# A selective-scan kernel: operand addresses on GpSimd, and a fixed order of products and scans on VectorE

## The chip, the core and the metric

The kernel runs on one core of a Trainium2 chip. A core has engines that work side by side, each through its own queue in order: TensorE (matrix products, PE in the profile), VectorE (DVE), ScalarE (ACT), GpSimd (POOL) and SyncE (SP), which issues transfers. They share a memory of 128 partitions, from which and to which the transfers go, and PSUM, into which TensorE writes and which VectorE and ScalarE read. The metric is the time of one execution on the device in microseconds; lower is better.

## What is computed

Two layers of a vision model on `x`, of shape (2, 96, 96, 96). The change lies in layer 0. There, after a normalisation over the channels, an input projection makes 192 channels of `xin` and a gate `z`; a 3x3 convolution, a GELU and a 1x1 convolution give an offset at each pixel, at which `xin` is sampled bilinearly. The sampled image is cut into windows of 36 tokens, and over each a selective scan runs in four directions, with 16 states to each channel:

```python
def step(hst, inputs):
    ut, dt, bt, ct = inputs
    dA = jnp.exp(dt[..., None] * A)
    hst = hst * dA + (dt * ut)[..., None] * bt[:, :, None, :]
    y = jnp.einsum('bkdn,bkn->bkd', hst, ct)
    return (hst, y)
...
return jnp.moveaxis(ys, 0, -1) + Dv[None, :, :, None] * u
```

The four outputs are summed, normalised, multiplied with `silu(z)` and projected; a small feed-forward net with quantised weights follows. Layer 1 (an attention against averaged cells, a 5x5 depthwise convolution and another such net) is the same before and after.

## The kernel before

Layer 0 goes over the two images in 32 stripes of 6 rows (576 tokens). For each stripe there are three parts. The front (`_l0_front`) loads, normalises, projects, convolves, samples, and writes the step sizes `dl`, the products `du` of step and input, and the C coefficients `c_d` to device memory, from where they are read again with each row laid out over partitions. The scan (`_l0_scan`) is next, and the back (`_l0_back`) does the rest. Front of the next stripe, scan of this one and back of the one before run interleaved.

The scan of a stripe has 2 halves of the channels, 2 orders of the tokens (`o`) and 2 directions (`kk`), each a section (`_l0_section`); a section has 4 quarters `i` of the states, and a quarter two units `c`, each of 288 tokens. So there are 1024 quarters and 2048 units in all. A quarter first loads `cre` (C, repeated over partitions) and has ScalarE make `dA` for both units in three decays (L1041, 3072 in all). Each unit then takes five steps:

- spread (L1056, TensorE): B, repeated over partitions, into a `bp` buffer in PSUM; there are two such buffers
- product (L1060, VectorE): `bp` becomes `dur` times B, 864 elements a partition. The product of the first unit also waits by hand for the three decays of its quarter, and for GpSimd and TensorE to be done with the `h` buffers that this quarter will write
- scan (L1076, VectorE): the recurrence over `dA` and `bp`, into one of six `h` buffers. When it has ended, the `bp` buffer is free for a later spread
- times C (L1081, GpSimd): `h` times `cre`, in place
- fold (L1093, TensorE): sums `h` over states into `y`; three matmuls for the first unit and six for the second.

The same GpSimd queue holds, for each stripe, fourteen steps of the sampling (L625 to L631, `sample`), twenty-four of the softplus and the product `du` (L759 to L762, in `steps`, three for each of two orders), their marks (`memset`), and two products with `zs` and a sum in the back (L937, L883).

The order of the work is planned as the program is built. `_Plan` records each operation with an engine, an estimated cost, what it reads and writes, and a due time; `order` then picks, again and again, the operation that can start earliest, with due time as second key. An operation that needs one of another engine is taken to be ready a fixed time (`LAG`) after that one's end, by the engine that is to run it: 1.5 us for VectorE. The instructions of each engine stay in that order on the chip. The costs of GpSimd come from `_cost` and, for times C, from a number of its own.

A tile may be given `skip`: `_place` then takes a buffer longer by `lead` (or `skip`) elements and starts the tile `skip` elements in, that is 4 bytes each after an aligned place. Before, `h` has skip 2, 4, 8 or 1 by quarter, `zs` 12, `x1` 14, `x2` 9, and `e`, `du`, `r` and `dl` 0, 1, 2 and 6:

```python
ht = S.tile(P.rep, [128, NBL, H2], "h", P.nh, skip=(2, 4, 8, 1)[i], lead=8)
```

`cre` has none. Nothing fixes the order of products and scans but the plan: 1814 of the 2048 scans stand between their own product and another product.

Of the kernel before, what the change touches and what calls it, by code (L numbers as in the profile page):

```python
# [9 lines left out]
F32 = mybir.dt.float32  # L10
# [4 lines left out]
ALU = mybir.AluOpType  # L15
# [11 lines left out]
C = 96  # L27
HW = 96
# [62 lines left out]
class _Op:  # L91
    def __init__(self, eng, cost, run, due, tab):
        self.eng, self.cost, self.run, self.due, self.tab = eng, cost, run, due, tab
        self.deps, self.tiles, self.start, self.end = set(), [], None, None
        self.left, self.then, self.ready = 0, [], 0.0

SAME = 0.06  # L100
LAG = {"pe": 0.5, "dve": 1.5, "act": 0.6, "pool": 1.0, "sp": 1.5}


class _Plan:
# [6 lines left out]

    def tile(self, pool, shape, tag, bufs=1, dtype=F32, name=None, skip=None, lead=0):
        t = _Tile(self, pool, tag, bufs, shape, dtype, name or tag)
        t.skip, t.lead = skip, lead or skip
        return t
# [30 lines left out]
    def order(self):  # L146
# [13 lines left out]
        while len(out) < len(self.ops):  # L160
# [70 lines left out]
def _place(t, tag):  # L231

    if t.skip is None:
        return t.pool.tile(t.shape, t.dtype, tag=tag, name=t.name, bufs=1)
    n = math.prod(t.shape[1:])
    flat = t.pool.tile([t.shape[0], n + t.lead], t.dtype, tag=tag, name=t.name, bufs=1)
# [223 lines left out]
def _l0_front(k, P, S, f, x, b, s, at):  # L460
# [25 lines left out]

    xt, xin = temp([C, 8, HW], "xt"), S.tile(P.front, [C, 2, 8, HW + 2], "xin", 1)
    if lo > r0:
# [9 lines left out]
    )  # L498
    pool(8, lambda: nc.gpsimd.memset(xin.ap[:, :, :, 0 : HW + 2 : HW + 1], 0.0), (), (xin,))
    rows = lambda t, c: t.ap[:, 4 * c : 4 * c + 4, :].rearrange("p r w -> p (r w)")  # L500
# [41 lines left out]

    zs = f.zs = S.tile(P.hand, [C, 2, T], "zs", 2, skip=12)

# [17 lines left out]
    def convolve(oh, c):  # L562
        pc = ps("pc")

        def part(ih, tap):
            dy, dx = divmod(tap, 3)
            pe(H2, lambda: nc.tensor.matmul(  # L567
                pc.ap[:C, :H2],
                k.w_c1[:, ih, tap, oh * C : (oh + 1) * C],
                xin.ap[:, ih, 3 * c + dy : 3 * c + dy + 3, dx : dx + HW],  # L570
                start=(ih == 0 and tap == 0),
                stop=(ih == 1 and tap == 8),
            ), (xin,), (pc,), (t,))
# [14 lines left out]

    fr = temp([C, 2, WIN, HW], "fr", 5)

# [24 lines left out]
    xs1 = S.tile(P.front, [C, 2, T], "xs1", 1)  # L615
    dif, top, bot = temp([C, 2, 7, HW], "dif"), temp([C, 2, WIN, HW], "top", 2), temp([C, 2, WIN, HW], "bot")
    g = nc.gpsimd
    tt = g.tensor_tensor

    def sample(half):  # L620
        v = lambda: xin.ap[:, half, 1:8, 1 : HW + 1]
# [3 lines left out]
        pool(672, lambda: tt(d(), xin.ap[:, half, 1:8, 2 : HW + 2], v(), ALU.subtract), (xin,), (D,))  # L625
        pool(T, lambda: tt(tp(), d()[:, 0:6], fx(), ALU.mult), (D, (fr, 1)), (TP,))
# [35 lines left out]
    def order_of(o, xs):  # L662
# [50 lines left out]

        x1, x2 = row("x1", 1, skip=14), row("x2", 1, skip=9)

# [14 lines left out]
        def steps(m):  # L730
# [277 lines left out]
def _l0_section(k, P, S, f, first, o, h, kk, py, at, tau):  # L1008
# [41 lines left out]
    def unit(u, i, c, cre, dA, t0):  # L1050
        toks = slice(c * H2, (c + 1) * H2)
        bp = S.tile(P.ps, [128, 1024], "bp", 2)
        ht = S.tile(P.rep, [128, NBL, H2], "h", P.nh, skip=(2, 4, 8, 1)[i], lead=8)

# [16 lines left out]
        def scan():  # L1071
            hv, dv = (v.rearrange("p b n -> p (b n)") for v in (ht.ap, dA.ap[:, c]))
            bv = bp.ap[:, : NBL * H2]
            if kk:
                hv, dv, bv = hv[:, ::-1], dv[:, ::-1], bv[:, ::-1]
            nc.vector.tensor_tensor_scan(hv, dv, bv, 0.0, ALU.mult, ALU.add)  # L1076

        S.op("dve", 2.0, scan, (dA, bp), (ht,), due=t0 + (1.35 - P.early["dve"]) * tau)

        def times_c():  # L1080
            nc.gpsimd.tensor_tensor(  # L1081
                ht.ap, ht.ap, cre.ap[:, toks].unsqueeze(1).to_broadcast([128, NBL, H2]), ALU.mult)
            P.issued["pool", u] = latest()

        S.op("pool", 2.06, times_c, (cre,), (ht,), due=t0 + (2.3 - P.early["pool"]) * tau)

        def states():
            end = o == 1 and kk == 1 and i == NQ - 1

            def part(dst, v, stop):  # L1090
                if o:
                    v = v.rearrange("p (w j i) -> p w i j", i=WIN, j=WIN)
                nc.tensor.matmul(dst, k.fold, v, start=False, stop=stop)  # L1093

            for blk in range(NBL):
                dst = py.ap[CB * blk : CB * blk + CB]
                n = HEAD - H2 if c else H2
                part(dst[:, c * H2 : c * H2 + n], ht.ap[:, blk, :n], end and c == 1)
            if c:
                for blk in range(NBL):  # L1100
                    part(_tail(py, blk), ht.ap[:, blk, n:], end and blk == NBL - 1)
            P.issued["pe", u] = latest()

        S.op("pe", 1.0, states, (ht,), (py,), due=t0 + (3.5 - P.early["pe"]) * tau)

# [4 lines left out]
def _layer0(k, tc, a, x, x2d):  # L1110
# [3 lines left out]
    with ExitStack() as st:  # L1114
# [852 lines left out]
```

## Time and profile before

| | |
|---|---|
| three runs, us | 8442.23 (median), 8434.59, 8457.52 |
| the profiled execution, us | 8449.37; span 8447.6 |
| granted TensorE clock, mean | 0.907 |
| first product to the end of the last scan | 145.3 to 6391.7 us |
| VectorE busy, 1000 to 6000 us | 96.7 to 97.8 of each 100 |
| GpSimd busy, same | 89.9 to 90.7 |
| TensorE busy, same | 85.8 to 86.9 |
| ScalarE busy, same | 77.1 to 77.9 |
| DMA busy, same | 0.48 to 0.49 |

The page first gives the busy time of each engine with its share of the span; then the span in 40 slices with the busy tenths of each; then the costliest groups of instructions. A group's line names the source line, engine, operation, tiles out and in, shapes and count; after the bar stand busy time in us and the mean of one in ns, then the idle time just before these instructions and what ended most of it. A timeline's line has start, length, engine, line, operation, tiles, shapes and count, and in brackets the idle time before it and its releaser. A line of the table of waits has who waited for whom, the sum in us, the number of times and the longest. A duration can overlap the next instruction's by some tens of ns.

### The profile page before, as it was taken

To read this page: it belongs to the slowest core of one execution; us is meant where nothing else is said; L and a number is where in the kernel's file an instruction comes from. 1 tells how busy PE (TensorE), PEld (TensorE's weight loads), DVE (VectorE), ACT (ScalarE), POOL (GpSimd) and SP (SyncE) were. 2 spreads that over 40 slices of the span, in tenths; PEclk is the share of its full clock that TensorE was granted. 3 is DMA by queue.
4 is the path that set the end of the run, shared out by engine and by line. 5 is a ranking of instruction groups with operands and counts; after the bars stand their busy time and mean duration, and the time that the engine had idled before them with its cause. 6 is when DMAs were issued, how large, how long until landed. Compare 5 with 4: busy or idle time off the path is not lost. (4 is left out here: it accounts for less than half of the span.)

```text
span 8447.6 us, 118902 instructions
## 1 busy us (share of the span) xinstructions
PE 7320.6 (87%) x43653; PEld 3406.4 (40%) x43653; DVE 7806.9 (92%) x5398; ACT 6339.6 (75%) x10688; POOL 5742.1 (68%) x3835
## 2 busy tenths in 40 slices
PE   7888888888888888888888888888857999989998
PEld 4444444444444444444444444444423223542245
DVE  3999999999999999999999999999996998959988
ACT  5777777777777777787777877787745886778867
POOL 4999989888889889999988999999873000110001
PEclk8898989999899889999989998999867999989999
DMA  2444444444444444444444444444442000110001
GB/s 89 142 153 152 152 154 150 149 153 146 148 151 149 149 148 153 155 151 150 155 152 147 149 153 150 152 154 155 147 135 63 3 2 14 36 48 3 2 22 33
DMA packets 339992, 985.62 MB, mean 117 GB/s; under 512 B 50152, under 2 KB 51872, under 8 KB 339104
## 3 DMA queue, kind: packets, MB, share of 16 engines
q1 hardware_dynamic: 337488, 977.74, 37.1%
q8 instruction: 347, 5.69, 0.3%
q14 instruction: 253, 2.07, 0.1%
q10 hardware_dynamic: 1904, 0.12, 0.0%
HBM read 797.19 MB, written 139.25 MB: 111 GB/s over the span
## 5 line engine op out<-in xcount | busy, mean ns | idle before, releaser
L1081 POOL TENSOR_TENSOR h<-h,cre 128x864 f32<-128x864 f32 x2048 | 3965.5, 1947 | 616.1 <-DVE h L1076 357.4
L1076 DVE TENSOR_TENSOR_SCAN h<-dA,bp 128x864 f32<-128x864 f32 x2048 | 3996.8, 1953 | 105.4 <-PE y L1093 27.2
L1041 ACT ACTIVATE dA<-dlr,A 128x576 f32<-128x576 f32 x3072 | 2156.5, 765 | 886.1 <-DVE h L1076 828.6
L1060 DVE TENSOR_TENSOR bp<-dur,bp 128x864 f32<-128x864 f32 x2048 | 2133.6, 1043 | 132.9 <-PE bp L1056 51.1
L1093 PE MATMUL y<-h,fold 128*32 128x288 f32 (+2 forms) x18432 | 1841.2, 446 | 154.4 <-POOL h L1081 152.6
L567 PE MATMUL pc<-xin,off 96*96 96x288 f32 x4608 | 1328.1, 420 | 0.0
L1056 PE MATMUL bp<-bt,selb 128*128 128x288 bf16 x2048 | 644.1, 316 | 700.4 <-DVE h L1076 683.7
L1429 ACT ACTIVATE pr<-sc 128x960 f32<-128x960 f32 (+1 forms) x1080 | 954.0, 937 | 202.8 <-PE sc L1425 182.5
L1093 PEld LDWEIGHTS y<-h,fold 128*32 128x32 f32 x18432 | 755.0, 117 | 857.6 <-issue 376.1
L1509 DVE TENSOR_TENSOR sums<-sums,pr 128x3840 f32<-128x3840 f32 (+1 forms) x240 | 959.0, 3996 | 56.9 <-ACT pr L1429 34.7
L567 PEld LDWEIGHTS pc<-xin,off 96*96 96x96 f32 x4608 | 705.2, 165 | 497.8 <-issue 247.2
L1601 POOL MEMSET vch<- 96x32 f32 x16 | 2.4, 152 | 1304.6 <-DVE dist L1463 1213.4
L1056 PEld LDWEIGHTS <-selb 128*128 128x128 bf16 x2048 | 201.5, 99 | 1455.9 <-DVE h L1076 1231.0
L1425 PE MATMUL sc<-qH,kH 32*128 32x480 f32 (+1 forms) x3240 | 627.2, 602 | 10.4 <-DMA q<-qH 5.6
L1425 PE MATMUL sc<-q,kH 32*128 32x480 f32 (+1 forms) x1080 | 564.7, 602 | 0.0
L1491 PE MATMUL av<-pr,vT 128*32 128x480 f32 (+1 forms) x4320 | 533.4, 564 | 3.6 <-ACT av L1516 3.5
L1682 DVE SCALAR_TENSOR_TENSOR acc<-vch,lepe_w,acc 96x1152 f32<-96x1152 f32 x320 | 469.0, 1466 | 7.9
L1425 PEld LDWEIGHTS sc<-qH,kH 32*128 32x128 f32 x3240 | 219.0, 184 | 419.7 <-issue 223.8
L883 POOL TENSOR_TENSOR x<-x,fy 96x576 f32<-96x576 f32 x32 | 53.3, 1664 | 479.1 <-ACT fy L882 415.1
L740 PE MATMUL pt<-xd,w_dt 96*128 96x288 f32 x768 | 304.1, 492 | 21.7 <-ACT xin L532 10.6
L761 POOL TENSOR_TENSOR dl<-dl,r 128x576 f32<-128x576 f32 x192 | 270.9, 1411 | 9.1 <-ACT dl L758 4.1
L762 POOL TENSOR_TENSOR du<-dl,x 128x576 f32<-128x576 f32 x192 | 271.7, 1415 | 6.6
(270 smaller groups left out, 9902.7 us busy)
## 6 DMA issues: line engine op xcount, KB each, us to landing
cre<-c_d SPq DMA_DIRECT2D x1024, 288.0 KB
dur<-du_d SPq DMA_DIRECT2D x256, 864.0 KB
dlr<-dl_d SPq DMA_DIRECT2D x256, 864.0 KB
x<-xs SPq DMA_DIRECT2D x512, 72.0 KB
du_d<-du SPq DMA_DIRECT2D x128, 288.0 KB
dl_d<-dl SPq DMA_DIRECT2D x128, 288.0 KB
du_d<-du SPq DMA_DIRECT2D x128, 144.0 KB
dl_d<-dl SPq DMA_DIRECT2D x128, 144.0 KB
```

Of the source, the lines that this page charges most:

```text
L567: pe(H2, lambda: nc.tensor.matmul(pc.ap[:C, :H2], k.w_c1[:, ih, tap, oh * C : (oh + 1) * C], xin.ap[:, ih, 3 * c + dy : 3 * c + dy + 3, dx ...
L1041: nc.scalar.activation(dA.ap[:, :, blk, :], dlr.ap[:, blk, :].rearrange("p (c n) -> p c n", c=2), AF.Exp, scale=k.A[:, i, kg, h, blk : blk ...
L1056: nc.tensor.matmul(bp.ap[:, :H2], k.selb[:, kk, i, :], f.bc[o].ap[:, toks], start=True, stop=True)
L1060: nc.vector.tensor_tensor(bp.ap[:, : NBL * H2].rearrange("p (b n) -> p b n", b=NBL)[:, ::-1], dur.ap[:, ::-1, toks], bp.ap[:, :H2].unsquee ...
L1076: nc.vector.tensor_tensor_scan(hv, dv, bv, 0.0, ALU.mult, ALU.add)
L1081: nc.gpsimd.tensor_tensor(ht.ap, ht.ap, cre.ap[:, toks].unsqueeze(1).to_broadcast([128, NBL, H2]), ALU.mult)
L1093: nc.tensor.matmul(dst, k.fold, v, start=False, stop=stop)
L1425: nc.tensor.matmul(two[to // 2][:, to % 2, :n], kH[rows, k0 : k0 + 128], q, start=True, stop=True)
L1429: nc.scalar.activation(pr[:, 2 * i : 2 * i + 2, :n], two[i][:, :, :n], AF.Exp, scale=HD**-0.5)
L1491: nc.tensor.matmul((main if s < HEADS else other)[s * HD : (s + 1) * HD, :n], vT[:, blk, hd, :], pr[:, place(s, p), :n], start=at == 0, st ...
L1509: nc.vector.tensor_tensor(both, both, pr[:, :, :, :n], ALU.add)
L1682: S.op("dve", 1.43, lambda: nc.vector.scalar_tensor_tensor(acc.ap, src(), W.lw[:, t : t + 1], acc.ap, ALU.mult, ALU.add), (vch,), (acc,))
```

## The change

It has two parts. First, the tiles that GpSimd reads in pairs are moved so that the two operands start 8 bytes apart modulo 16 where that can be had: `h` has skip 2 in all quarters, against `cre` with none; `zs`, `x1`, `x2` and `du` have skip 2, `dl` and `e` 0, `r` stays at 2; `fr` and `top` move; `xin` is two columns wider and its pixels begin one column later. In the built program every times C, softplus step, `du` and `zs` product is then at 8 bytes; the sampling steps are at 8, 4 or 12. Before, times C was at 8 bytes in quarter 0, at 0 in quarters 1 and 2 and at 12 in quarter 3. `lead` is gone.

Secondly, each product and scan also writes a token, `P.turn`, in the order in which they are recorded, and a quarter's first scan, times C and fold are recorded only after its second product. So VectorE has product, product, scan, scan in each quarter, and the quarters one after another; other VectorE work may still stand between. The planner's costs change along: product 1.03 to 1.0, times C 2.06 to 1.75, GpSimd's `_cost`, and 0.6 us instead of 1.5 from a spread to its product (`SOON`).

```diff
+SOON = {"dve": 0.6}
...
-                p.ready = max(p.ready, o.end + (SAME if p.eng == o.eng else LAG[p.eng]))
+                p.ready = max(p.ready, o.end + (SAME if p.eng == o.eng else o.lag[p.eng]))
...
-        return 0.1 + 0.00235 * cols
+        return 0.2 + 0.00177 * cols
...
-    xt, xin = temp([C, 8, HW], "xt"), S.tile(P.front, [C, 2, 8, HW + 2], "xin", 1)
+    xt, xin = temp([C, 8, HW], "xt"), S.tile(P.front, [C, 2, 8, HW + 4], "xin", 1)
...
-            xin.ap[:, half, 4 * c : 4 * c + 4, 1 : HW + 1],
+            xin.ap[:, half, 4 * c : 4 * c + 4, 2 : HW + 2],
...
-    zs = f.zs = S.tile(P.hand, [C, 2, T], "zs", 2, skip=12)
+    zs = f.zs = S.tile(P.hand, [C, 2, T], "zs", 2, skip=2)
...
-    fr = temp([C, 2, WIN, HW], "fr", 5)
+    fr = temp([C, 2, WIN, HW], "fr", 2)
...
-    dif, top, bot = temp([C, 2, 7, HW], "dif"), temp([C, 2, WIN, HW], "top", 2), temp([C, 2, WIN, HW], "bot")
+    dif, top, bot = temp([C, 2, 7, HW], "dif"), temp([C, 2, WIN, HW], "top", 1), temp([C, 2, WIN, HW], "bot")
...
-        x1, x2 = row("x1", 1, skip=14), row("x2", 1, skip=9)
+        x1, x2 = row("x1", 1, skip=2), row("x2", 1, skip=2)
...
-            e, du, r, w = (row(name, 2, skip=n) for name, n in (("e", 0), ("du", 1), ("r", 2), ("dl", 6)))
+            e, du, r, w = (row(name, 2, skip=n) for name, n in (("e", 0), ("du", 2), ("r", 2), ("dl", 0)))
...
-        ht = S.tile(P.rep, [128, NBL, H2], "h", P.nh, skip=(2, 4, 8, 1)[i], lead=8)
+        ht = S.tile(P.rep, [128, NBL, H2], "h", P.nh, skip=2)
...
-        S.op("pe", 0.3, spread, (f.bc[o],), (bp,), due=t0 - P.early["pe"] * tau)
-        S.op("dve", 1.03, product, (dur,), (bp,), due=t0 - P.early["dve"] * tau)
...
-        S.op("dve", 2.0, scan, (dA, bp), (ht,), due=t0 + (1.35 - P.early["dve"]) * tau)
...
-        S.op("pool", 2.06, times_c, (cre,), (ht,), due=t0 + (2.3 - P.early["pool"]) * tau)
...
+        S.op("pe", 0.3, spread, (f.bc[o],), (bp,), due=t0 - P.early["pe"] * tau).lag = SOON
+        S.op("dve", 1.0, product, (dur,), (bp, P.turn), due=t0 - P.early["dve"] * tau)
+
+        def rest():
...
+            S.op("dve", 2.0, scan, (dA, bp), (ht, P.turn), due=t0 + (1.35 - P.early["dve"]) * tau)
...
+            S.op("pool", 1.75, times_c, (cre,), (ht,), due=t0 + (2.3 - P.early["pool"]) * tau)
...
+        if c == 0:
+            P.behind = rest
+        else:
+            P.behind()
+            rest()
...
+        P.turn, P.behind = S.held(k.ident, "turn"), None
```

In the built program each engine has as many instructions as before but ScalarE, which has 78 more: loads of function tables, since the plan orders its work otherwise.

More of the change, by code (lines that the diff above doesn't have):

```diff
@@ L110, in __init__, with tile @@
         self.rate = {}
-    def tile(self, pool, shape, tag, bufs=1, dtype=F32, name=None, skip=None, lead=0):
+    def tile(self, pool, shape, tag, bufs=1, dtype=F32, name=None, skip=None):
         t = _Tile(self, pool, tag, bufs, shape, dtype, name or tag)
-        t.skip, t.lead = skip, lead or skip
+        t.skip = skip
         return t
@@ L235, in _place @@
     n = math.prod(t.shape[1:])
[L236 removed]
+    flat = t.pool.tile([t.shape[0], n + t.skip], t.dtype, tag=tag, name=t.name, bufs=1)
     v, d = flat[:, t.skip : t.skip + n], t.shape[1:]
@@ L1104, in unit, with scan, times_c, states @@
-        S.op("pe", 1.0, states, (ht,), (py,), due=t0 + (3.5 - P.early["pe"]) * tau)
+        S.op("pe", 0.3, spread, (f.bc[o],), (bp,), due=t0 - P.early["pe"] * tau).lag = SOON
+        S.op("dve", 1.0, product, (dur,), (bp, P.turn), due=t0 - P.early["dve"] * tau)
+        def rest():
+            def scan():
+                hv, dv = (v.rearrange("p b n -> p (b n)") for v in (ht.ap, dA.ap[:, c]))
+                bv = bp.ap[:, : NBL * H2]
+                if kk:
+                    hv, dv, bv = hv[:, ::-1], dv[:, ::-1], bv[:, ::-1]
+                nc.vector.tensor_tensor_scan(hv, dv, bv, 0.0, ALU.mult, ALU.add)
+            S.op("dve", 2.0, scan, (dA, bp), (ht, P.turn), due=t0 + (1.35 - P.early["dve"]) * tau)
+            def times_c():
+                nc.gpsimd.tensor_tensor(
+                    ht.ap, ht.ap, cre.ap[:, toks].unsqueeze(1).to_broadcast([128, NBL, H2]), ALU.mult)
+                P.issued["pool", u] = latest()
+            S.op("pool", 1.75, times_c, (cre,), (ht,), due=t0 + (2.3 - P.early["pool"]) * tau)
+            def states():
+                end = o == 1 and kk == 1 and i == NQ - 1
+                def part(dst, v, stop):
+                    if o:
+                        v = v.rearrange("p (w j i) -> p w i j", i=WIN, j=WIN)
+                    nc.tensor.matmul(dst, k.fold, v, start=False, stop=stop)
+                for blk in range(NBL):
+                    dst = py.ap[CB * blk : CB * blk + CB]
+                    n = HEAD - H2 if c else H2
+                    part(dst[:, c * H2 : c * H2 + n], ht.ap[:, blk, :n], end and c == 1)
+                if c:
+                    for blk in range(NBL):
+                        part(_tail(py, blk), ht.ap[:, blk, n:], end and blk == NBL - 1)
+                P.issued["pe", u] = latest()
+            S.op("pe", 1.0, states, (ht,), (py,), due=t0 + (3.5 - P.early["pe"]) * tau)
```

33 lines of the change are left out of this document (5 added, 28 removed).

## The prediction

> **What bounds the kernel now.** I read the page's busy shares and slices first, to see which engine fills which part of the span; then the costliest groups, for prices; then the timelines of VectorE and GpSimd, for how one instruction follows another; then the table of waits.
>
> ```profile
> PE 7320.6 (87%) x43653; PEld 3406.4 (40%) x43653; DVE 7806.9 (92%) x5398; ACT 6339.6 (75%) x10688; POOL 5742.1 (68%) x3835
> ...
> DVE  3999999999999999999999999999996998959988
> ...
> POOL 4999989888889889999988999999873000110001
> ...
> L1081 POOL TENSOR_TENSOR h<-h,cre 128x864 f32<-128x864 f32 x2048 | 3965.5, 1947 | 616.1 <-DVE h L1076 357.4
> L1076 DVE TENSOR_TENSOR_SCAN h<-dA,bp 128x864 f32<-128x864 f32 x2048 | 3996.8, 1953 | 105.4 <-PE y L1093 27.2
> ...
> L1060 DVE TENSOR_TENSOR bp<-dur,bp 128x864 f32<-128x864 f32 x2048 | 2133.6, 1043 | 132.9 <-PE bp L1056 51.1
> ```
>
> VectorE is full from the first slice to the thirtieth, which is layer 0, and its rows there are 2048 products and 2048 scans. GpSimd stands at 8 and 9 tenths beside it. The scans run from 145.3 to 6391.7 us, that is 6246 us for 1024 quarters of two units each. All edits lie in layer 0, so what follows (2056 us) stays.
>
> VectorE's timeline, one instruction or merged run per line (start, length):
>
> ```profile
> 955.23 1.04 DVE L1060 TENSOR_TENSOR bp<-dur,bp 128x864 f32<-128x864 f32 x1
> 956.30 1.95 DVE L1076 TENSOR_TENSOR_SCAN h<-dA,bp 128x864 f32<-128x864 f32 x1
> 958.17 1.04 DVE L1060 TENSOR_TENSOR bp<-dur,bp 128x864 f32<-128x864 f32 x1
> 959.25 1.95 DVE L1076 TENSOR_TENSOR_SCAN h<-dA,bp 128x864 f32<-128x864 f32 x1
> 961.12 2.00 DVE L1060 TENSOR_TENSOR bp<-dur,bp 128x864 f32<-128x864 f32 x2
> 963.03 3.79 DVE L1076 TENSOR_TENSOR_SCAN h<-dA,bp 128x864 f32<-128x864 f32 x2
> 968.07 1.06 DVE L1060 TENSOR_TENSOR bp<-dur,bp 128x864 f32<-128x864 f32 x1 [1.25 <-PE bp L1056]
> ```
>
> A scan right after its own product starts 0.03 us after the product's end; any instruction that does not need the one before it starts 0.08 to 0.09 us before that one's end. Two units in the order product, scan, product, scan take 5.89 us (955.23 to 961.12). The pair at 961.12 is in the order of the change: 1.91 us to its first scan, then 3.79 less the overlap of 0.08, in all 5.62. It then waited 1.25 us for a spread (L1056), which must be kept in mind.
>
> GpSimd's timeline over two instructions of quarter 3 (skip 1), two of quarter 0 (skip 2) and two of quarter 1 (skip 4):
>
> ```profile
> 4039.99 2.03 POOL L1081 TENSOR_TENSOR h<-h,cre 128x864 f32<-128x864 f32 x1 [0.90 <-PE fph L855]
> 4042.97 2.04 POOL L1081 TENSOR_TENSOR h<-h,cre 128x864 f32<-128x864 f32 x1 [0.96 <-PE pc L567]
> 4045.97 1.72 POOL L1081 TENSOR_TENSOR h<-h,cre 128x864 f32<-128x864 f32 x1 [0.96 <-PE pc L567]
> 4048.86 1.72 POOL L1081 TENSOR_TENSOR h<-h,cre 128x864 f32<-128x864 f32 x1 [1.16 <-DVE h L1076]
> 4051.86 2.03 POOL L1081 TENSOR_TENSOR h<-h,cre 128x864 f32<-128x864 f32 x1 [1.29 <-PE pc L567]
> 4054.75 2.04 POOL L1081 TENSOR_TENSOR h<-h,cre 128x864 f32<-128x864 f32 x1 [0.85 <-DVE h L1076]
> ```
>
> The same multiply takes 1714 ns in the 512 units with skip 2 and 2023, 2026 and 2023 ns at skips 4, 8 and 1. Only skip 2 puts `h` 8 bytes from `cre` modulo 16. The waits:
>
> ```profile
> PEld L1056 <- DVE h L1076: 1231.0, 1281, 3.4
> ...
> ACT dA L1041 <- DVE h L1076: 828.6, 537, 4.9
> ...
> PEld y L1093 <- POOL h L1081: 312.2, 357, 3.2
> ```
>
> TensorE and ScalarE wait for VectorE, TensorE's folds also for GpSimd. VectorE's own idle time inside the scans is small: its gaps above 60 ns sum to 132 us.
>
> **The change, part by part.** The sum is against the profiled execution's 8449.4 us; the median of the three runs is 7 us below it.
>
> *Order on VectorE.* With medians in ns, a quarter now costs 2 x (1042 + 34 + 1954 - 84) = 5892. In the new order it costs (1042 - 93) + (1053 - 93) + (1947 - 84) + (1928 - 84) = 5616, from the 29 such quads in the trace of before. So 276 ns a quarter, times 1024, is **-283 us**. Nearly all of it is the two waits of a scan for its own product. VectorE's 184 other instructions in the scans stay, about 0.08 us in each quarter on average, so the pace is 5.70 us.
>
> *The new wait.* There are two `bp` buffers. The second spread of a quarter may start only when the quarter before has ended its second scan, and its product is due one product later. TensorE, when it stands waiting, loads weights 53 ns after a scan's end and starts the spread at 57; the spread takes 297 and a waiting product starts 38 later: 392 ns after the scan's end. The product is due 949 - 84 = 865 ns after it. So 0.47 us is to spare; in the old order it was about 2.5 us. All else in TensorE's queue stands behind the waiting spread. The changed program puts 1.2 us of other TensorE work between a quarter's two spreads on average, against the 1.84 us of the scan that runs meanwhile. Matmuls of 96x288 f32 go at 482 ns each (two records 241 apart). Only the runs of `L948` and `L951` (five or six matmuls, some 30 quarters, 2.9 us) exceed 1.84 + 0.47 less the spread's 0.13: 0.7 us each, **+21**. If the 57 blocks of `L982` and `L984` took their six matmuls one after another they would exceed it too: 63; the low end is 0.
>
> *GpSimd.* 1536 multiplies drop by 309 ns (475 us); `L761` and `L762` fall from about 1413 ns to the 1206 of `L759` and `L760`, whose operands are 4 and 8 bytes apart (79 us); 64 of `L937` likewise (13 us). None of it is on VectorE, so it counts for nothing by itself: VectorE hides it. Its worth is what it keeps from turning into a wait. With the rows less the 35 ns overlap, GpSimd's work between second multiplies was 5.46 us a quarter and becomes 4.90, but unevenly: 340 quarters hold more than 5.70, and the fullest four in a row average 7.6. In the changed order both folds (L1093) of a quarter always stand ahead of the first spread of the quarter after the next, 3 or 4 spreads behind their own; before, it was 3 to 8. From a quarter's second scan, GpSimd ends after 1.8 us, the fold takes 0.57, and the spread that stands behind it must start by 5.15. That leaves 2.7 us, or 2.2 after the 0.44 us of other matmuls that stand there on average. A running sum of GpSimd's backlog against 5.70 a quarter, in which what exceeds 2.2 us stops VectorE, gives **+123**. With 4 us to spare it is 20, with 1.5 it is 168; I take 2.2 as the counted one.
>
> A rule speaks against this part. The Trainium skill, "GPSIMD Engine Reference", section "Instruction dispatch", calls about 2.5 cycles an element the floor of a two-input body; with its 1.2 GHz that is an estimated 1800 ns for 864 elements. The row of 1714 ns is under that, so the measurement decides. By the rule the backlog would be some 226 us instead of 123, and the sum about 100 us higher.
>
> *ScalarE.* The three decays go from ending before a product 5.89 us on to one 5.62 on. Its rows give 4.66 us a quarter in the changed order (4.57 before; the new order has 78 more table loads at 1.28 us). 160 quarters hold over 5.70. The decays have 3.5 us to spare, which costs 0. But TensorE's fillers read ScalarE's results, and there the spare time is 0.47 plus the 0.6 that the average stretch between the spreads leaves. The running sum at 1.0 us gives **+41**; ends 0 and 89.
>
> *Layout and rest.* `xin` two columns wider, other skips, `fr` and `top` shifted, `lead` gone: the same instructions on the same shapes. Scans take 1954 ns at all four skips of the `h` they write, so VectorE doesn't feel it. GpSimd's 448 sample steps have rows of 1201 to 1305 ns and may move within them, 45 us either way, which lies beside VectorE: 0, with ends -10 and +10 through the backlog. SP issues the same 2949 transfers, DMA is at 0.48 busy, `cre` has four buffers and `dlr`, `dur` a section's lead: 0.
>
> The stalls counted, 21 + 123 + 41 = 185, take the place of the 132 now there. Sum: -283 + 185 - 132 = -230, so 8449 - 230 = 8219, and 7 lower as a median: **8212 us**.
>
> **The rivals.** *The short round trip fails (slower).* If the second product came late as a rule, the order would lose. It decides where the mean lateness passes 0.28 us a quarter (plus what other stalls rise by). For it: of the 29 quads in the trace, 11 are followed by a wait such as that of 1.25 us above, in all 8.5 us, 0.29 a quad; folds now block the queue at 0.87 us a wait (312.2 over 357). If every quarter paid 0.87 - 0.47 = 0.40, that is +410 for -283: 8442 + 127 = 8569. Against: those quads stand in a queue written for the other order, and TensorE waits for scans 1281 times at L1056, so it mostly stands ready.
>
> *GpSimd or ScalarE takes over in bursts (little gained).* If GpSimd did not get faster, its running sum is 318: -283 + 21 + 318 + 41 - 132 = -35, 8407. The same number comes out if it does and the queues block each other at the tighter ends, 63 + 168 + 89 = 320: -95, 8347. For it: 9 tenths in the slices. Against: 1714 ns, 512 times.
>
> *Nothing measurable.* The gain of 283 meets stalls of 415: 8442.
>
> *All stalls fade.* Only 20 remain: -283 + 20 - 132 = -395, 8047; hardly.
>
> **How the numbers follow.** Near the sum, 8130 to 8330: 0.62. Still less stall, below 8130: 0.06. Little gained, 8330 to 8417: 0.12. Within 0.3% (25 us, about what a measurement of this kernel can tell from no change): 0.05. Slower, the round trip: 0.15. So faster 0.80, same 0.05, slower 0.15. The range reaches from 8090 to 8430 and leaves about 0.2 out, most of it above; the likeliest case has 8130 to 8330.
>
> **What would show it.** Multiply row near 1714 with all skips alike; `L761`, `L762` near 1206; POOL near 5170 us busy. In VectorE's timeline the two products of a quarter start 0.95 apart and its scans 1.86, while the rows of both keep their means within 15 ns. Waits of the product for `bp` (51 us now) would rise; if they rise past 300 us the round trip was mispriced. Waits of folds for GpSimd above 500 us would mean that its bursts bind. The clock granted to TensorE stays near 0.9 in layer 0, or its matmuls stretch and every term on TensorE with it.

## The result: 1.4% slower, and the profile after

The changed kernel takes 8561.7 us (median of 4 runs, 8555.3 to 8574.4) beside 8445.2 us for the kernel before on the same chip: a ratio of 1.014, 95% interval 1.0124 to 1.0156. Forecast was 8212, so the sign was wrong. The profiled execution has a span of 8559.0 us and a mean granted TensorE clock of 0.890 (0.907 before).

The page of the changed kernel: busy time, share of the span and instructions of each engine, then slices, then groups.

```profile
PE 7395.2 (86%) x43653; PEld 3414.5 (40%) x43653; DVE 7652.4 (89%) x5398; ACT 6417.1 (75%) x10766; POOL 5184.7 (61%) x3835
...
DVE  3999999999999999999999999999996998959988
...
POOL 4877877787777777888777877777864000110001
PEclk8988999988888888988888888888867999989999
...
L1083 POOL TENSOR_TENSOR h<-h,cre 128x864 f32<-128x864 f32 x2048 | 3493.4, 1713 | 1279.0 <-DVE h L1078 460.6
L1078 DVE TENSOR_TENSOR_SCAN h<-dA,bp 128x864 f32<-128x864 f32 x2048 | 3880.7, 1936 | 6.1 <-ACT dA L1042 6.1
...
L1061 DVE TENSOR_TENSOR bp<-dur,bp 128x864 f32<-128x864 f32 x2048 | 2093.8, 1049 | 507.7 <-PE bp L1057 464.2
```

Everything that the change was to do, it did. GpSimd's multiply takes 1713 ns in all quarters (1947 on average before) and GpSimd is busy for 5185 us (5742). The scans wait for next to nothing: 6.1 us, 105.4 before. But the products now wait for 507.7 us, 132.9 before, and 464.2 of it is put down to the spread (L1057; L1056 before). VectorE has 154 us less to do and still needs longer. The slices hide this: the DVE row is all nines in both kernels, since 9 stands for nine tenths or more.

VectorE's timeline in the changed kernel (start, length, engine, line and so on, idle time before and its releaser in brackets):

```profile
949.38 1.06 DVE L1061 TENSOR_TENSOR bp<-dur,bp 128x864 f32<-128x864 f32 x1 [1.24 <-PE bp L1057]
952.25 1.06 DVE L1061 TENSOR_TENSOR bp<-dur,bp 128x864 f32<-128x864 f32 x1 [1.81 <-PE bp L1057]
953.23 3.79 DVE L1078 TENSOR_TENSOR_SCAN h<-dA,bp 128x864 f32<-128x864 f32 x2
956.93 0.72 DVE L929 TENSOR_TENSOR Y<-Y,yva 96x576 f32<-96x576 f32 x1
957.58 2.02 DVE L1061 TENSOR_TENSOR bp<-dur,bp 128x864 f32<-128x864 f32 x2
959.51 3.79 DVE L1078 TENSOR_TENSOR_SCAN h<-dA,bp 128x864 f32<-128x864 f32 x2
963.22 2.00 DVE L1061 TENSOR_TENSOR bp<-dur,bp 128x864 f32<-128x864 f32 x2
965.13 3.79 DVE L1078 TENSOR_TENSOR_SCAN h<-dA,bp 128x864 f32<-128x864 f32 x2
968.83 2.00 DVE L1061 TENSOR_TENSOR bp<-dur,bp 128x864 f32<-128x864 f32 x2
```

From 957.58 on this is the quarter that was wanted: 957.58 to 963.22 is 5.64 us and 963.22 to 968.83 is 5.61. The quarter at 949.38 is the other kind: each of its two products stood waiting for its spread, 3.05 us in all, as much as twelve quarters gain by the new order (258 us over 1024, below).

What TensorE did in that quarter, by its own timeline:

```profile
944.95 0.69 PE L1095 MATMUL y<-h,fold 128*32 128x288 f32 x6 [0.63 <-POOL h L1083]
946.62 0.58 PE L1095 MATMUL y<-h,fold 128*32 128x216 f32 x12 [0.98 <-POOL h L1083]
947.13 0.92 PE L909 MATMUL yc<-Y,minus_mean 96*96 96x288 f32 x2
947.84 1.17 PE L909 MATMUL yc<-Y,less_mean 96*96 96x288 f32 x2
948.80 0.45 PE L1057 MATMUL bp<-bt,selb 128*128 128x288 bf16 x1
949.04 1.17 PE L640 MATMUL px<-top,ident 96*96 96x288 f32 x2
950.00 1.12 PE L640 MATMUL px<-bot,ident 96*96 96x288 f32 x2
950.96 0.65 PE L640 MATMUL px<-top,ident 96*96 96x288 f32 x2
951.45 0.65 PE L640 MATMUL px<-bot,ident 96*96 96x288 f32 x2
951.93 0.29 PE L1057 MATMUL bp<-bt,selb 128*128 128x288 bf16 x1
```

TensorE waited twice for GpSimd, at its folds (L1095); then it worked without a pause, and the first spread (L1057 at 948.80) and the second (951.93) stood behind other matmuls. And the same matmuls have two lengths: a pair of L640 takes 1.17 and then 0.65 us, a spread 0.45 and 0.29. The windows of the trace show why. Columns: stretch in us, its length, then busy time and (count) of PE, PEld, DVE, ACT and POOL, the granted TensorE clock, DMA share and GB/s.

```profile
944.12:947.53 3.41, 1.79 (x21) 0.88 (x21) 3.41 (x3) 0.42 (x2) 3.41 (x3) 1.00 0.01 3
947.53:950.95 3.42, 3.42 (x9) 1.93 (x8) 1.67 (x2) 2.25 (x5) 3.34 (x5) 0.50 0.25 86
950.95:954.36 3.41, 3.41 (x28) 1.72 (x26) 2.10 (x2) 2.80 (x7) 1.46 (x1) 1.00 0.21 33
```

In the first stretch TensorE was busy for 1.79 of 3.41 us; in the next its clock is 0.50; it is busy all through that, and the clock is 1.00 again. The clock's records hold these two values alone, in multiples of 3.41 us.

The waits of the changed kernel (who waits for whom, us in total, times, longest):

```profile
PEld L1057 <- DVE h L1078: 834.7, 909, 2.5
PEld y L1095 <- POOL h L1083: 707.6, 767, 3.7
...
DVE bp L1061 <- PE bp L1057: 464.2, 481, 3.6
...
PE y L1095 <- POOL h L1083: 268.7, 369, 2.8
```

Before, the spread's weight load waited for scans 1281 times; now 909 times. So it arrives late at the spread more often instead of standing ready in front of it.

For what follows I sum VectorE's stalls from its timeline: the idle time ahead of each product and scan beyond its normal spacing, where it is over 0.1 us. The scans (first product to last scan) took 6246 us before, with stalls of 129 us: 6117 without them. After, 6371 us with 512 us: 5859 without. So **the order gained 258 us and the stalls took back 383**. Of the 512 us, 378 lie ahead of a quarter's second product (364 times) and 134 ahead of its first (136 times), and in 495 of these 500 a spread was the last to arrive. Outside the scans the span is within 14 us of before.

### The profile page after: what moved, and what is told of

It is laid out like the page before. It is cut to its first block, busy times and chain, and to the rows that moved or that the text cites. A ratio compares the mean times of both kernels' runs of the same rounds, so it can differ in the third digit from the quotient of the medians.

```text
span 8559.0 us, 118883 instructions
## 1 busy us (share of the span) xinstructions
PE 7395.2 (86%) x43653; PEld 3414.5 (40%) x43653; DVE 7652.4 (89%) x5398; ACT 6417.1 (75%) x10766; POOL 5184.7 (61%) x3835
## 3 DMA queue, kind: packets, MB, share of 16 engines
q14 instruction: 251, 2.06, 0.1%
## 5 line engine op out<-in xcount | busy, mean ns | idle before, releaser
L1083 POOL TENSOR_TENSOR h<-h,cre 128x864 f32<-128x864 f32 x2048 | 3493.4, 1713 | 1279.0 <-DVE h L1078 460.6
L1078 DVE TENSOR_TENSOR_SCAN h<-dA,bp 128x864 f32<-128x864 f32 x2048 | 3880.7, 1936 | 6.1 <-ACT dA L1042 6.1
L1061 DVE TENSOR_TENSOR bp<-dur,bp 128x864 f32<-128x864 f32 x2048 | 2093.8, 1049 | 507.7 <-PE bp L1057 464.2
L1095 PE MATMUL y<-h,fold 128*32 128x288 f32 (+2 forms) x18432 | 1847.6, 449 | 274.2 <-POOL h L1083 268.7
L568 PE MATMUL pc<-xin,off 96*96 96x288 f32 x4608 | 1365.9, 422 | 5.3 <-ACT xin L533 5.2
L1095 PEld LDWEIGHTS y<-h,fold 128*32 128x32 f32 x18432 | 754.3, 120 | 1265.6 <-POOL h L1083 707.6
L1057 PE MATMUL bp<-bt,selb 128*128 128x288 bf16 x2048 | 653.0, 322 | 537.8 <-DVE h L1078 533.2
L1057 PEld LDWEIGHTS <-selb 128*128 128x128 bf16 x2048 | 208.7, 102 | 1026.9 <-DVE h L1078 834.7
L741 PE MATMUL pt<-xd,w_dt 96*128 96x288 f32 x768 | 344.8, 539 | 100.5 <-ACT zs L551 62.0
L746 ACT ACTIVATE e<-pt,dt_b 128x288 f32<-128x288 f32 x384 | 191.3, 498 | 176.0 <-PE pt L741 172.4
```

The source lines that it names most:

```text
L568: pe(H2, lambda: nc.tensor.matmul(pc.ap[:C, :H2], k.w_c1[:, ih, tap, oh * C : (oh + 1) * C], xin.ap[:, ih, 3 * c + dy : 3 * c + dy + 3, dx ...
L1057: nc.tensor.matmul(bp.ap[:, :H2], k.selb[:, kk, i, :], f.bc[o].ap[:, toks], start=True, stop=True)
L1061: nc.vector.tensor_tensor(bp.ap[:, : NBL * H2].rearrange("p (b n) -> p b n", b=NBL)[:, ::-1], dur.ap[:, ::-1, toks], bp.ap[:, :H2].unsquee ...
L1083: nc.gpsimd.tensor_tensor(ht.ap, ht.ap, cre.ap[:, toks].unsqueeze(1).to_broadcast([128, NBL, H2]), ALU.mult)
```

## The experiments

The theories. One: the fixed order fails by itself, because the second spread has too little time (the rival that the prediction called the short round trip). Two: the order is sound, and something else in the change spoils it. The planner's new costs are part of the change, and they write the queues anew.

### The parts alone

`pairs_only` has the new addresses and GpSimd's new planner costs, and VectorE's order is left to the plan:

```diff
-        S.op("dve", 1.0, product, (dur,), (bp, P.turn), ...)
+        S.op("dve", 1.03, product, (dur,), (bp,), ...)
...
-            S.op("dve", 2.0, scan, (dA, bp), (ht, P.turn), ...)
+            S.op("dve", 2.0, scan, (dA, bp), (ht,), ...)
```

> The first half of the change alone: all tiles and GpSimd costs as changed, but products and scans in the free order of before, with the old product cost and the old 1.5 us lag. Theory one (the second product's short round trip through TensorE costs more than the order gains): GpSimd's multiplies go to 1714 ns, the product's waits for its spread stay near the 51 us of before, and the time is that of before or a little less, 8380 to 8450. Theory two (the new planner costs reorder the other queues badly, and the fixed order is innocent): 8500 or more, with waits for spreads above 300 us.

Measured: 8400.7 us, 0.9938 [0.9918, 0.9958]. Stalls 74 us, scans without them 6132.

`order_only` has the fixed order with the old tiles and the old `_cost` and times C cost:

> The second half alone: product, product, scan, scan with its token, product cost and lag, but tiles and GpSimd costs of before. Theory one: the spread waits of 464 us are here too, and GpSimd at 1947 ns a multiply adds to them, 8560 to 8750. Theory two: without the new GpSimd costs the order gains, below 8440.

Measured: 8356.3 us, 0.9888 [0.9870, 0.9907]. Its waits:

```profile
PEld y L1095 <- POOL h L1083: 1305.9, 1208, 3.0
...
PE y L1095 <- POOL h L1083: 584.9, 726, 2.6
```

Theory one is out: the fixed order by itself makes the kernel faster. Its stalls are 295 us, its scans without them 5861. Note that folds wait for GpSimd for 1891 us here, nearly twice as long as in the changed kernel (976 us), and it is 205 us faster. The sign that the prediction named for "its bursts bind", more than 500 us of these waits, does not tell a good queue from a bad one.

Both parts gain alone, and together they lose. What both halves share is the planner, which orders all queues anew for each.

### The token in the other order

`psps_fixed` is the whole change, but a quarter's order is product, scan, product, scan, and the spread's lag is 1.5 us again:

```diff
-        S.op("pe", 0.3, spread, (f.bc[o],), (bp,), ...).lag = SOON
+        S.op("pe", 0.3, spread, (f.bc[o],), (bp,), ...)
...
-        if c == 0:
-            P.behind = rest
-        else:
-            P.behind()
-            rest()
+        rest()
```

> All of the change, but the token fixes product, scan, product, scan instead; the lag from spread to product is 1.5 us again. Theory one: a product then has a product and a scan of time for its spread, so waits for spreads fall below 100 us and the time is that of before, 8390 to 8460. Rival (any strict order costs, as the planner can no longer move a late unit behind an early one): 8520 or more.

Measured: 8398.2 us, 0.9940 [0.9921, 0.9959]; stalls 77 us, 6130 without them. So neither the token nor the new costs do harm in this order; it is as good as `pairs_only` and no better.

### The planner's costs against the addresses

`after_oldcosts` is the whole change, planned with GpSimd's old costs:

```diff
-        return 0.2 + 0.00177 * cols
+        return 0.1 + 0.00235 * cols
...
-            S.op("pool", 1.75, times_c, ...)
+            S.op("pool", 2.06, times_c, ...)
```

> The whole change, but the planner is told GpSimd's old costs (2.06 us for times C, 0.1 + 0.00235 us a column). Every engine then has its instructions in the order of order_only; only the addresses differ. Theory three (the new planner costs make a TensorE order that, with the fixed order on VectorE, crowds the spreads): 8280 to 8350, no slower than order_only, waits of products for spreads at most 200 us, and the half-clock share of TensorE as in order_only, 0.15 to 0.20. Rival (the new addresses clash with the fixed order on the chip): 8500 or more.

`order_newcosts` is its counterpart, the old tiles planned with the new costs:

> The fixed order with the old addresses, but the planner is told the new GpSimd costs. Every engine then has its instructions in the order of the changed kernel. Theory three: at least as slow as the changed kernel, 8560 to 8850, since GpSimd is slower still. Rival (addresses): near order_only, 8340 to 8400.

Each engine has the same instructions in the same order in `after_oldcosts` and `order_only`, and likewise in `order_newcosts` and the changed kernel. So the four make a square in which either the addresses or the planner's two costs change:

| fixed order, us | planned with old costs | planned with new costs |
|---|---|---|
| old addresses | 8356.3 | 8745.8 |
| new addresses | **8211.1** | 8561.7 |

`after_oldcosts` has a ratio of 0.9720 [0.9701, 0.9739]: faster than both kernels, below the 8280 to 8350 that was expected of it, and 1 us from the forecast of the whole change. `order_newcosts` has 1.0353 [1.0333, 1.0374], as theory three expected. The addresses gain 145 and 184 us by the columns. The planner's two numbers cost 351 to 390. They change the order of the queues and no instruction but ScalarE's loads of function tables: 440 in the changed kernel, 330 in `after_oldcosts`. These loads are not the cause: `timesc_old` (below) has 330 too and is 190 us slower than `after_oldcosts`. Of `after_oldcosts` the page's first line and its wait for spreads:

```profile
PE 7087.9 (86%) x43653; PEld 3300.6 (40%) x43653; DVE 7630.2 (93%) x5398; ACT 6274.4 (76%) x10656; POOL 5180.5 (63%) x3835
```

```profile
DVE bp L1061 <- PE bp L1057: 123.9, 205, 3.7
```

and of `order_newcosts`:

```profile
DVE bp L1061 <- PE bp L1057: 565.2, 536, 3.9
```

TensorE's 43653 matmuls take 7088 us in the one and 7395 us in the changed kernel: the same matmuls, 307 us longer.

### Which of the two numbers

`timesc_old` takes back 1.75 for times C alone, `cost_old` takes back `_cost` alone:

> The whole change, but the planner is told times C's old cost, 2.06, while `_cost` keeps its new formula; so of the two new GpSimd costs only one is left. Known by now: both old gives 8211, both new 8562. Theory one: the harm comes from 1.75 for times C, which stands in every unit and places folds and spreads in TensorE's queue, so taking it back alone restores the gain: 8190 to 8270, waits of products for spreads of 110 to 180 us. Theory two: it comes from `_cost`, which moves the sampling and softplus steps and with them TensorE's other work: 8450 to 8600, waits above 350 us. If both are needed for the harm, this run and the next are both near 8211; if either is enough, both are near 8560.

> The whole change, but `_cost` goes back to its old formula, while times C is planned at its new 1.75. Theory one (times C's number does the harm): 8450 to 8600, waits of products for spreads above 350 us. Theory two (`_cost` does it): 8190 to 8270, waits of 110 to 180 us.

Measured: 8400.8 us, 0.9946 [0.9929, 0.9962], and 8338.9 us, 0.9874 [0.9857, 0.9890]. Both theories missed. Each number does part of the harm: 128 us by 1.75 alone, 190 us by `_cost` alone, 351 us together.

`pairs_oldcosts` has the new addresses, and every engine's order as before:

> The addresses alone: the kernel before with the tiles of the changed one, and every cost and the order on each engine as before. GpSimd's rows fall (times C to 1714) and nothing else is changed. If GpSimd's slower rows held up VectorE in the old order only by the waits that the run with the new costs also lost, 8390 to 8410, as in that run (8401). If the planner's new costs made its order worse there too, as they do in the fixed order, this run is below it: 8300 to 8380. If GpSimd was fully hidden in the order of before, 8440 to 8455.

Measured: 8439.5 us, 0.9992 [0.9983, 1.0002]. In the old order GpSimd was fully hidden: 3497 us of times C instead of 3966 move nothing. So by the faster GpSimd alone nothing is gained there; what `pairs_only` gained came with its newly planned order.

### A cost too low, or another deal

If costs set too low do the harm, higher ones should do none. `timesc_high` plans times C at 2.3 and keeps the old `_cost`; `cost_high` plans times C at 2.06 with `_cost` 0.1 + 0.0029 * cols.

> The whole change with `_cost` at its old formula and times C planned at 2.3, above both the old number (2.06) and what the chip takes (1.71). By now 1.75 gives 8339 and 2.06 gives 8211. If a cost set too low does the harm in one direction (the planner puts folds and what hangs on GpSimd too early), more is no worse: 8190 to 8250, waits of products for spreads of 90 to 160 us. If each set of costs merely deals another order, and 2.06 was a lucky one, this lies among the other three fixed orders: 8300 to 8500, waits of 200 to 450 us.

> The whole change with times C planned at 2.06 and `_cost` raised to 0.1 + 0.0029 * cols, above the old formula as that is above the new one. One direction: 8190 to 8250, waits of 90 to 160 us. Another order dealt, and the old one lucky: 8300 to 8500, waits of 200 to 450 us.

Measured: 8400.7 us, 0.9941 [0.9924, 0.9957], and 8397.5 us, 0.9941 [0.9925, 0.9958], with waits for spreads of 296.8 and 283.4 us. That is the second case of the expectation: each set of costs deals another order. The old set is the best of the six with the new addresses and the new set the worst; whether the old one is best by luck or by fit isn't shown. All runs with the fixed order side by side ("clock at half" is the share of the stretch from 1000 to 6000 us in which the clock's record is 0.5; "excess" is explained below):

| fixed order | time | scans | stalls | scans less stalls | clock at half | excess at full clock | excess as it ran |
|---|---|---|---|---|---|---|---|
| `after_oldcosts` | 8211 | 6018 | 162 | 5856 | 0.167 | 9 | 22 |
| `cost_old` | 8339 | 6154 | 298 | 5856 | 0.190 | 8 | 50 |
| `order_only` | 8356 | 6156 | 295 | 5861 | 0.153 | 9 | 19 |
| `cost_high` | 8398 | 6216 | 354 | 5863 | 0.206 | 16 | 90 |
| `timesc_high` | 8401 | 6206 | 350 | 5856 | 0.222 | 19 | 86 |
| `timesc_old` | 8401 | 6202 | 346 | 5857 | 0.257 | 8 | 71 |
| the change | 8562 | 6371 | 512 | 5859 | 0.246 | 28 | 97 |
| `order_newcosts` | 8746 | 6552 | 690 | 5862 | 0.261 | 28 | 94 |

The scans less their stalls are the same to 7 us. All that tells these kernels apart is the stalls.

"Excess" is the prediction's own count of the new wait: for each quarter the matmuls that stand between its two spreads, and what they exceed 2.18 us by (1.84 for the scan and 0.47 to spare, less 0.13), summed. With each matmul at its full-clock duration (the lower quartile of its kind) it gives 8 to 28 us. With the durations of the trace it gives 19 to 97. Even that is not the stalls' size, for it leaves out waits, and it takes the first spread of a quarter to be on time. In the changed kernel that spread starts 0.40 us after its scan's end in the median, and more than 0.47 us after it in 41 of 100 quarters; in `after_oldcosts` 0.06 us, and 20 of 100. This share does not rank the kernels either: `timesc_old` has 43 of 100 and is 161 us faster than the change. `order_only` has the queues of `after_oldcosts` and differs only by GpSimd's slower rows. Its stalls are 295 us against 162, and the way is by the folds: they wait for GpSimd for 1891 us there, and here for 716:

```profile
PEld y L1095 <- POOL h L1083: 546.5, 610, 3.1
...
PE y L1095 <- POOL h L1083: 169.8, 313, 2.8
```

### The clock

Two kernels were to make TensorE's queue short, at the cost of a wrong output: in `before_short` and `after_short` 17 of 18 convolution matmuls have 32 columns and the folds 36 columns a block.

```diff
-                pc.ap[:C, :H2],
+                pc.ap[:C, : (32 if ih + tap else H2)],
...
-                part(dst[:, c * H2 : c * H2 + n], ht.ap[:, blk, :n], end and c == 1)
+                part(dst[:, c * H2 : c * H2 + SEQ], ht.ap[:, blk, :SEQ], end and c == 1)
```

> The kernel before, with the same order on all queues, but less TensorE work: 17 of the 18 matmuls of each convolution block cover 32 columns instead of 288, and each fold's matmuls 36 columns a block. The output is not the model's. Theory one (spreads come late because TensorE is still on other work): the few waits for spreads shrink, 8350 to 8440.

> The changed kernel, same order on all queues, with the same shortened TensorE work; the output is not the model's. Theory one: TensorE's clock is nearly always full in layer 0 and the products' waits for spreads fall from 464 us to between 100 and 200, so it is faster than the shortened kernel before by 60 to 250 us: 8150 to 8320. Rival (the fixed order itself, or a wait on another engine through TensorE's queue, costs the time): waits stay above 350 us and the time above 8450.

Measured: 8514.4 us, 1.0076 [1.0056, 1.0096], and 8617.5 us, 1.0196 [1.0176, 1.0217]. Both expectations of a gain missed: with less to do on TensorE both kernels are slower than their full versions. The page's clock slices and a window of 5000 us of `before_short`:

```profile
PEclk6555555555655556565655555555557999989999
```

```profile
1000.00:6000.00 5000.00, 3966.37 (x25075) 2334.95 (x25074) 4789.67 (x3389) 3822.86 (x6606) 4432.92 (x2892) 0.59 0.48 149
```

The clock is at half for 0.83 of that stretch (0.18 in the kernel before). A spread, which was left as it is, takes 422 ns in the median while the clock is at half and 296 ns while it is full. So the pair does not settle what it was built for: `after_short` has the rival's numbers (waits for spreads of 502.5 us, a time above 8450), but its clock fell along with its queue.

This suggests a rule for the fall of the clock, and the records bear it out. I cut the stretch from 1000 to 6000 us into the clock's own pieces of 3.41 us and took TensorE's busy share in each. In the changed kernel, of 174 pieces at full clock after which it fell to half, 95 of 100 had a busy share under 0.60; of 929 after which it stayed, 95 of 100 had over 0.65. The kernel before shows the same borders (0.62 and 0.68). For the return there is no such border: of the 174 half-clock pieces after which the changed kernel's clock came back the median busy share is 1.00, and so it is of the 186 after which it stayed at half. What brings it back stays open. The Trainium skill, "TensorE: Matmul & The Clock Gate", section "HAM oscillation — how this bites in real kernels", gives as the rule that TensorE should not stand idle for more than about 3.4 us. Here keeping to it is no safeguard: between 1000 and 6000 us TensorE's longest idle time in the changed kernel is 2.28 us, and its clock fell 174 times. Several shorter waits in a piece do it.

So late spreads could be the half clock's work. To tell, I gave TensorE *more* work where it would wait: one matmul against zeros a quarter, ahead of the first unit's fold.

```diff
+                if c == 0:
+                    nc.tensor.matmul(
+                        py.ap[:CB, :288], k.none, cre.ap[:, :288], start=False, stop=False)
                 for blk in range(NBL):
```

> The changed kernel with one more matmul in each quarter: ahead of the first unit's fold, 288 columns of `cre` against a block of zeros, added to `y`, which leaves `y` as it is. It costs TensorE about 0.48 us at full clock, 493 us over the scans; no engine's order is otherwise changed. In the records the clock falls to half at the end of a stretch of 3.41 us in which TensorE was busy for less than about 0.6, and comes back after one in which it was nearly always busy. Theory one (idle stretches lower the clock, and the lower clock makes the spreads late): the half-clock share of 1000 to 6000 us falls from 0.246 to under 0.15, VectorE's stalls from 512 us to 200 to 400, time 8250 to 8450, although TensorE has more to do. Theory two (the clock is a consequence, the queue's contents alone are late): stalls grow to 550 to 750, 8600 to 8800.

> The same with 144 columns, 0.24 us a quarter at full clock. Theory one: between, share 0.14 to 0.22, 8350 to 8510. Theory two: 8570 to 8680.

> The 288 columns of zeros in the best order so far (the whole change, planned with the old GpSimd costs, 8211). Theory one: half-clock share from 0.167 to under 0.10, stalls from 162 us to 80 to 160, 8120 to 8210. Theory two: 8250 to 8400.

> The 144 columns in that order. Theory one: 8150 to 8210. Theory two: 8220 to 8300.

| us | time | ratio to before | clock at half | stalls while at full clock | stalls while at half |
|---|---|---|---|---|---|
| the change | 8561.7 | 1.0140 [1.0124, 1.0156] | 0.246 | 244 | 275 |
| `after_warm_half` | 8507.4 | 1.0080 [1.0062, 1.0097] | 0.152 | 322 | 147 |
| `after_warm` | 8560.2 | 1.0147 [1.0129, 1.0165] | 0.107 | 408 | 90 |
| `after_oldcosts` | 8211.1 | 0.9720 [0.9701, 0.9739] | 0.167 | 140 | 27 |
| `oldcosts_warm_half` | 8224.0 | 0.9742 [0.9724, 0.9759] | 0.129 | 158 | 23 |
| `oldcosts_warm` | 8283.2 | 0.9813 [0.9792, 0.9833] | 0.093 | 216 | 18 |

(The last two columns are summed by the clock's record at the stall, with slightly other edges than the sums above.) The added work in `after_warm`, and its clock:

```profile
PEclk8999999999999999999999999999977999989999
```

```profile
L1100 PE MATMUL y<-cre,none 128*32 128x288 f32 x2048 | 750.2, 451 | 0.0
```

More work does keep the clock up: the share at half falls from 0.246 to 0.152 and 0.107. The stalls that fall in half-clock time go from 275 to 147 and 90 us. With 144 columns the kernel is 54 us faster than the change although TensorE has 1024 matmuls more; the two intervals do not meet. All queues are otherwise in the same order, and what the added matmul does by its length alone is to cost time, as the good order shows (8224 and 8283 us for 8211). So the half clock is a cause and not only a companion. But the 288 columns cost as much as they bring, since they stand in the queue like any other work (750 us busy; the profile counts each as two records), and in the good order, where only 27 us of stalls fell in half-clock time, both sizes only cost. Theory one's clock shares were all met. Of its times only that of the 144 columns in the changed kernel's order was, and just; in the good order both times are theory two's, and `after_warm` is neither's. Nor did the stalls fall as far as theory one had it: 498 us in `after_warm` for 200 to 400, and 234 us in `oldcosts_warm` for 80 to 160. Each theory is half of it.

How large each half is can only be estimated. At full clock the changed kernel stalls for 244 us in the 4695 us of its scans with that clock, 52 us in 1000; had it stalled at that rate throughout its 6371 us, that would be 331 us, an estimate. So about 180 of the 350 us by which it stalls more than `after_oldcosts` go with the half clock, though not all of them need be caused by it, since waits also bring the half clock on. The rest is the queue's order, which at full clock too stalls nearly twice as much (52 against 29 us in 1000).

What stays open: which feature of a plan makes it good. Work between two spreads, counted at full clock, does not tell the six with the new addresses apart in the order of their times (8 to 28 us). A third `bp` buffer, which might take the wait away, wasn't tried.

## Why the prediction was wrong, point by point

- **Order on VectorE, -283 us.** The mechanism and the rows held: a quarter at 5.61 to 5.64 us where nothing is late, no scan waiting for its own product. Measured is 6117 to 5859, -258. The sum took all 1024 quarters of before as product, scan, product, scan, though only 1814 of 2048 scans stood between their own product and another one; 283 times that share is 251.
- **The new wait, +21 (0 to 63).** This step failed. Stalls ahead of second products are 378 us (32 before) and ahead of first ones 134 (64 before). The step made two assumptions that failed. It took every first spread to start when its scan ends; its median lateness is 0.40 us, and in 41 of 100 quarters it is more than the 0.47 us that were to spare. And it took all matmuls at 482 ns, the full-clock length; the same count at the lengths that they had gives 97 us instead of 28. How the 512 us of stalls divide between the two isn't measured; about 180 us go with the half clock by the estimate above. The clause that "its matmuls stretch and every term on TensorE with it" if the clock falls was there as a sign to look for, and its price was not in the range.
- **GpSimd, +123 and nothing by itself.** The rows came out as read: 1713 ns for 1714, L761 and L762 (now L762 and L763) at 1205 for 1206, 5185 us busy for 5170. That the gain is worth nothing in the old order is shown by `pairs_oldcosts` (0.9992), and that it is worth much in the new one by the square: 145 and 184 us, where the difference of the two running sums, 318 and 123, is 195. But the stalls that end at GpSimd directly come to 3 us. Its bursts reach VectorE as waits of folds ahead of a spread, the same path as the term above, so the terms are not a sum of separate things.
- **ScalarE, +41.** One stall, of 6 us, ended at a decay. On the path that the step named, TensorE's matmuls waiting for ScalarE, the waits over 0.15 us within the scans sum to 163 us (89 before); `after_oldcosts` has 188, so they don't make the difference between the two. What they cost by themselves can't be separated from the rest of the queue here.
- **Layout, 0.** Right: `pairs_oldcosts` takes 8439.5 us for 8445.3. (The transfers of SyncE are the same in number, as the step says, but each trace holds 2923 and not 2949.)
- **Stalls in all, 185.** Measured 512 for the change, and 162 in `after_oldcosts`, whose time is the forecast's to 1 us. That closeness is partly luck: there the order gained some 260 us and not 283, and the stalls were fewer than summed by about as much. The sum priced an average order of this kind, and came out at the best of the eight. The plan that was to run is one deal out of many, and they lie between 8211 and 8562 with the new addresses.
- **The rivals.** The short round trip, 8569 by 0.40 us a quarter, has the measured time, and its own threshold fits: stalls are 0.50 us a quarter. It held a chance of 0.15 for the reason that quads in the old trace stood "in a queue written for the other order". That was the weak point: the new queue could be read off the built program, and it was weighed by its averages only. But the round trip is not late as a rule: 500 stalls of about 1 us make the sum, and the rest runs at the priced pace. The sign it gave, waits past 300 us, came in at 464.

## What to carry to other kernels

When an edit changes a planner's costs along with the code, run the code with the old costs too: here the numbers alone were worth 4%, against 3% for the edit, and a more truthful cost gave a worse plan. When a change cuts the spare time of a round trip through an in-order queue, count the queue as the clock will run it, with the work ahead of the first transfer, not only between the two. And when you fix one engine's order, look at the queues that feed it: VectorE's own time gained nearly what was counted (258 of 283 us), and lost more (383 us) in waits for what it is fed by.

## What the runs showed of the hardware that was not expected

- TensorE's clock fell to half after 3.41 us in which it was busy for less than about 0.6, without any long idle time: in the changed kernel after all 107 pieces with a share under 0.50, 57 of 91 from 0.50 to 0.60, and 1 of 882 above 0.65. So less work can be slower (8514 us for 8455, in the kernel before with short matmuls), and a matmul against zeros can pay for itself (8507 for 8562).
- The time of the two-input multiply on GpSimd depends on the addresses of its operands: in one kernel and one queue order (`order_newcosts`) 864 elements a partition take 1713 ns in the 512 units at 8 bytes apart modulo 16, and 2019 ns in the 1536 at 0 or 12. With all units at 8 bytes and the same order (the change) all take 1713 ns.
